# A three-pass float32 convolution network on one core: longer DRAM rows for three intermediate tensors, and the last pass's first layer in two halves instead of three thirds

## The chip, the cores and the metric

The kernel runs on one NeuronCore of a Trainium2 chip. The metric is the device time of one execution in microseconds. All data are float32. Engines are named as the profile names them: PE is TensorE's matmul, PEld its weight load, DVE VectorE, ACT ScalarE, POOL GpSimd, SP SyncE.

## What is computed

The input x is 8 x 96 x 96 x 192 (image, row, column, channel). Two residual layers follow, each on a group-normalised copy of its input (32 groups per image).

```
# layer 0
p     = gn(x) @ W_in + b_in                       # 192 -> 384
local = depthwise 3x3 conv(p)
mixed = local + 0.25 * (four running averages of local along rows and columns)
x1    = x + (layernorm(mixed) * g + b) @ W_out + b_out     # 384 -> 192
# layer 1
y     = depthwise 7x7 conv(gn(x1)) + bias
y     = gelu(layernorm(y) @ w0 + b0)              # 192 -> 768
x2    = x1 + gamma * (y @ w1 + b1)                # 768 -> 192
```

## The kernel before, in words

The program is one function, `conv_blocks_kernel`, with five stages one after the other; each writes an intermediate tensor to DRAM that the next one reads. The order of the instructions of each engine is the order of the program text (`tc.manual_schedule()`), and semaphores are put in where one engine's result is another's input or where a buffer is used again.

1. Projection (to about 750 us): group statistics of x, transposes, W_in, store to `P_d`.
2. The 3x3 convolution and the running averages (to about 1840 us): `P_d` to `M_d`.
3. LayerNorm and W_out (to about 2910 us): `M_d` to x1, which is stored twice. `finish_c` stores the sum in pixel order to `X2_d` (rows of 48 KB: one per image pair, column residue modulo 3 and image row), 3 KB of a row at a time from 96 partitions. `store_c` stores the channel-first copy `x1c` to `X1_d` (rows of 48 KB, every third one for one residue, so 144 KB from partition to partition), 3 KB of a row at a time. The last row of `X1_d` is a row of zeros, written in stage 1 from `pad`.
4. The 7x7 convolution (about 2910 to 3500 us): 16 rounds. `load_d` brings six channels of `X1_d` into `xin`, in runs of 1536 B: 64 rows, 48 KB apart, into partitions 0 to 63 by SyncE, and 64 more into partitions 64 to 127 by GpSimd; likewise the `band` of kernel weights. `scale_d` normalises on VectorE (L1009), `conv_d` runs the matmuls (L1024), ScalarE adds the bias into `yo` (L1035), and `store_d` writes `yo` to `Y_d` (L1064 from GpSimd; in the last round also L1063 from SyncE). A row of `Y_d` holds 4 image pairs x 2 column halves x 192 channels x 32 pixels, 192 KB, written in runs of 768 B.
5. The last pass (from about 3520 us): 24 loads of `y`, each 96 rows of 24 KB that lie 576 KB apart (L1116), and 96 units of 4 columns, four to a load. A unit u goes through these steps, which the loop at the end of the function interleaves over three neighbouring units:

   - `stats_e`, `norm_e`: LayerNorm of the unit on VectorE, with a power on GpSimd (L29)
   - `turn_in(u, k)`, k = 0, 1, 2: four transposes into one PSUM bank `pt` (L1169), which VectorE copies to `yT` (L1173)
   - `first_layer(u, mb)`, mb = 0, 1, 2: two of the six 128-column blocks of the hidden layer for both halves of the channels' pixels. The 192 channels are split as 128 + 64, so each of 4 sums, in a PSUM bank `hp` each, is a matmul over 128 rows (L1186) and one over 64 rows (L1196). The two 64-row matmuls of one block use different rows of the array. ScalarE then takes the GELU of each bank (L1205)
   - `second_layer(u, k)`, k = 0, 1, 2: 12 matmuls of 192 columns into one bank `po` (L1216), VectorE adds the residual `r` from `X2_d` (L1223), and GpSimd issues two stores of the output

   In the loop, thirds are interleaved: first_layer(u, k), turn_in(u + 1, k), statistics or norm of unit u + 2, second_layer(u - 1, k). [...] two for `pt`, four for `hp`, two for `po`.

A float32 matmul appears in the trace as two matmul records and two weight loads.

Of the kernel before, what the change touches and what calls it, by code (L numbers as in the profile page):

```python
# [8 lines left out]
F32 = mybir.dt.float32  # L9
# [3 lines left out]
PSUM = bass.MemoryType.PSUM  # L13
# [71 lines left out]
def conv_blocks_kernel(  # L85
# [31 lines left out]
    nc = tc.nc  # L117
    B, S, _, D = x.shape
# [4 lines left out]
    NE = EXP // 128  # L123
# [16 lines left out]
    PH = 3  # L140
    WV = S // PH

    X1_d = dram.tile([BP * S * PH + 1, D, WV, 2], F32, name="X1_d")
    X2_d = dram.tile([BP, PH, S, WV, 2, D], F32, name="X2_d")
    NV = 2
    WQ = WV // NV

    Y_d = dram.tile([S * PH, BP, NV, D, 2 * WQ], F32, name="Y_d")


    ZL = 2 * RB + 2
# [69 lines left out]
    with ExitStack() as ph:  # L221
# [68 lines left out]
        def store_kernels():  # L290
            nc.sync.dma_start(
                Z0_d.rearrange("(m p) t l -> p m (t l)", p=128),
                z0.rearrange("p m t l -> p m (t l)"),
            )

            nc.sync.dma_start(Z1_d.rearrange("(i c) p l -> c i p l", c=S), z1)
            nc.sync.dma_start(
                X1_d[BP * S * PH].rearrange("(i c) v b -> i (c v b)", i=S), pad
            )

        NK = RB // WA
# [435 lines left out]

    def load_d(m):
        c = m * HC
        row = D * WV * 2  # L740
        pool = d_pools[m % ND > 0]
        xin = pool.tile([128, NT, BP, HC, 2 * WV], F32, tag="xin", name="xin")

        for t in range(NT):
            for g, eng in enumerate((nc.sync, nc.gpsimd)):
                src = bass.AP(
                    tensor=X1_d.tensor,
                    offset=X1_d.offset + (2 * t + g) * HG * PH * row + c * WV * 2,
                    ap=[[row, 64], [S * PH * row, BP], [1, HC * WV * 2]],
                )  # L750
                eng.dma_start(
                    xin[g * 64 : (g + 1) * 64, t].rearrange("q a c n -> q a (c n)"), src
                )
        band = pool.tile([128, HC, ZW], F32, tag="band", name="band1")
        for g, eng in enumerate((nc.sync, nc.gpsimd)):
            eng.dma_start(
                band[g * 64 : (g + 1) * 64].rearrange("q c l -> q (c l)"),
                Z2_d[:, c : c + HC].rearrange("r c l -> r (c l)"),
            )
        return band, xin  # L760
# [4 lines left out]
    with ExitStack() as ph:  # L765
# [85 lines left out]
        def finish_c(x1c, part, w, pos, rs, xr):  # L851
            x1u = sp.tile([S, WB, 2, D], F32, tag="x1u", name="x1u", bufs=3)
            for j in range(WB):
                for b in range(2):
                    k = 2 * j + b
                    nc.vector.scalar_tensor_tensor(
                        x1u[:, j, b],
                        pos[j][:S, b, :D],
                        rs[:, k : k + 1],
                        xr[:, b, j],  # L860
                        ALU.mult,
                        ALU.add,
                    )

            nc.gpsimd.dma_start(
                X2_d[part // NH, part % NH, :, w : w + WB].rearrange("h v b c -> h (v b c)"),
                x1u.rearrange("h v b c -> h (v b c)"),
            )
            nc.vector.tensor_copy(
                x1c[:, :, w : w + WB].rearrange("h c v b -> h (v b) c"),  # L870
                x1u.rearrange("h v b c -> h (v b) c"),
            )
# [118 lines left out]
    with ExitStack() as ph:  # L991
# [51 lines left out]
        def store_d(yo, i):  # L1043
            for bl in range(NB):

                pieces = [(3, HB - 3)]
                if bl == 0:
                    pieces.append((HB - 3, HB))
                if bl == NB - 1:
                    pieces.append((0, 3))  # L1050
                for k in range(2):
                    c = i * CD + k * HC
                    for lo, hi in pieces:
                        r = (S - HB - bl * HG) * PH
                        src = yo[k * 64 + lo * PH : k * 64 + hi * PH, bl]
                        dst = Y_d[r + lo * PH : r + hi * PH, :, :, c : c + HC].rearrange(
                            "r b a c n -> r (b a) (c n)"
                        )
                        src = src.rearrange("r a c n -> r a (c n)")

                        n = NV if i == D // CD - 1 else 0
                        if n:
                            nc.sync.dma_start(dst[:, :n], src[:, :n])  # L1063
                        nc.gpsimd.dma_start(dst[:, n:], src[:, n:])  # L1064
# [25 lines left out]

    WH = 4
    WE = 2 * WH
    HE = 128 // WH
    with ExitStack() as ph:
        ip = ph.enter_context(tc.tile_pool(name="e_in", bufs=2))
        sp = ph.enter_context(tc.tile_pool(name="e_small", bufs=3))
        tp = ph.enter_context(tc.tile_pool(name="e_t", bufs=2))
        ps_t = ph.enter_context(tc.tile_pool(name="e_ps_t", bufs=2, space=PSUM))  # L1100
        ps_h = ph.enter_context(tc.tile_pool(name="e_ps_h", bufs=4, space=PSUM))
        ps_o = ph.enter_context(tc.tile_pool(name="e_ps_o", bufs=2, space=PSUM))

        def place(n):
            bp, n = divmod(n, PH * NV)
# [7 lines left out]
        def load_y(n):  # L1113
            bp, p, a = place(n)
            ys[n] = ip.tile([S, D, 2 * WQ], F32, tag="y", name=f"y_{n}")
            nc.sync.dma_start(ys[n], Y_d[PH - 1 - p :: PH, bp, a])  # L1116

        def load_r(u):
            n, t = divmod(u, per)
            bp, p, a = place(n)  # L1120
            v = a * WQ + t * WH
            rs_[u] = ip.tile([128, S // HE, 2 * D], F32, tag="r", name="r", bufs=4)
            for k in range(S // HE):
                nc.sync.dma_start(
                    rs_[u][:, k],
                    X2_d[bp, p, k * HE : (k + 1) * HE, v : v + WH].rearrange(
                        "h v b c -> h v (b c)"
                    ),
                )

        def bias_r(u):
            r = rs_[u].rearrange("p k (b c) -> p (k b) c", b=2)
            nc.gpsimd.tensor_tensor(
                r, r, b1g.unsqueeze(1).to_broadcast([128, 2 * S // HE, D]), ALU.add
            )
# [41 lines left out]
        def first_layer(u, mb):  # L1177
            if mb == 0:
                gs[u] = tp.tile([128, NE, 2, WH * S], F32, tag="g", name="g")
            yT, g = yTs[u].rearrange("p k h j -> p k (h j)"), gs[u]  # L1180
            ms = (2 * mb, 2 * mb + 1)
            hps = {}
            for m in ms:
                for q in range(2):
                    hps[m, q] = ps_h.tile([128, WH * S], F32, tag="hp", name="hp")
                    nc.tensor.matmul(  # L1186
                        hps[m, q],
                        w0w[:, 2 * q, m * 128 : (m + 1) * 128],
                        yT[:, 2 * q],
                        start=True,  # L1190
                        stop=False,
                    )
            for m in ms:
                for q in range(2):
                    p = slice(q * DH, (q + 1) * DH)
                    nc.tensor.matmul(  # L1196
                        hps[m, q],
                        w0w[p, 1, m * 128 : (m + 1) * 128],
                        yT[p, 1],
                        start=False,  # L1200
                        stop=True,
                    )
            for m in ms:
                for q in range(2):
                    nc.scalar.activation(  # L1205
                        g[:, m, q], hps[m, q], AF.Gelu, bias=b0g[:, m : m + 1], scale=1.0
                    )

        def second_layer(u, k):
            if k == 0:  # L1210
                xos[u] = tp.tile([128, S // HE, 2, D], F32, tag="xo", name="xo")
            g, xo = gs[u], xos[u]
            po = ps_o.tile([128, 2, D], F32, tag="po", name="po")
            for q in range(2):
                for m in range(NE):
                    nc.tensor.matmul(  # L1216
# [22 lines left out]
        with tc.manual_schedule():  # L1239
# [8 lines left out]
                    for k in range(3):  # L1248
                        turn_in(0, k)
            for u in range(n_u + 1):  # L1250
                for k in range(3):
                    if u < n_u:
                        first_layer(u, k)
                    if u + 1 < n_u:
                        turn_in(u + 1, k)
                    if k == 0:
                        if u + 1 < n_u:
                            load_r(u + 1)
                        if u < n_u:
                            bias_r(u)  # L1260
                    if u + 2 < n_u:
                        if k < 2:
                            for j in range(4 * k, 4 * k + 4):
                                stats_e(u + 2, j)
                        else:
                            for j in range(WE):
                                norm_e(u + 2, j)
                    if u >= 1:
                        second_layer(u - 1, k)


# [45 lines left out]
```

## Time and profile before

6009.42 us, the median of three runs (6007.35 to 6020.1). The profiled execution took 6009.9 us.

| engine | busy us | share of the span |
|---|---|---|
| PE | 5680.5 | 95% |
| PEld | 3943.4 | 66% |
| DVE | 3454.0 | 57% |
| POOL | 2634.7 | 44% |
| ACT | 2440.3 | 41% |

The costliest groups of the last pass on PE are L1216 (1178.3 us busy), L1186 (794.4 us) and L1196 (449.4 us). The page's slices show tenths of busy time per fortieth of the span (150 us each): PE is at 9 tenths or full everywhere but in the slices of the 7x7 convolution, where it is at 6 or 7, and the DMA engines are at 9 or full there. Matmul records overlap, since a matmul's end is modelled: what a matmul costs is read from the distance of the starts, and not from the durations. The table of windows gives busy time, granted clock and DMA traffic per stretch; its DMA share can go a little over 1.

### The profile page before, as it was taken

The page shows a single profiled execution, that of the slowest core. Times are in us where ns is not written, and L with a number is a line of the kernel's source. Part 1 is how long each engine was busy: PE and PEld are TensorE (multiplying, and loading weights), DVE is VectorE, ACT ScalarE, POOL GpSimd, SP SyncE. Part 2 cuts the span into 40 slices and gives each one's busy share as a digit, 9 for nine tenths or more (in the row PEclk, how much of TensorE's full clock was granted, in tenths as well). Part 3 has the DMA queues.
Part 4 walks back from the last instruction along what each step waited for, and adds up shares of the span by engine and source line. Part 5 has one row for each costly group of instructions (what it writes and reads, how often), then busy time and mean ns, then how long its engine had stood idle before and what let it go on. Part 6 is the DMA issues. An engine that isn't in the chain of part 4 may idle for free.

```text
span 6009.9 us, 122810 instructions
## 1 busy us (share of the span) xinstructions
PE 5680.5 (95%) x48550; PEld 3943.4 (66%) x48550; DVE 3454.0 (57%) x8023; ACT 2440.3 (41%) x6146; POOL 2634.7 (44%) x2835
## 2 busy tenths in 40 slices
PE   6999989999998999999677769999999999999999
PEld 3655633333336989898666657777777777777777
DVE  5555469999995667777532334444444444444442
ACT  2444457777774555555333322222222222222221
POOL 1111148888886666666444422322332233233222
PEclk9999989999999999999888889999999999999999
DMA  7999779999987888888899952222222222222221
GB/s 206 282 285 258 219 213 243 244 242 244 244 231 210 266 261 268 262 267 261 232 286 290 284 141 69 66 72 63 79 64 78 64 79 64 78 64 77 61 64 37
DMA packets 570206, 1054.36 MB, mean 175 GB/s; under 512 B 109575, under 2 KB 426260, under 8 KB 567328
## 3 DMA queue, kind: packets, MB, share of 16 engines
q1 hardware_dynamic: 439344, 593.23, 37.8%
q0 software_dynamic: 124160, 450.67, 24.1%
q8 instruction: 384, 6.29, 0.5%
q10 hardware_dynamic: 6128, 2.61, 0.2%
q14 instruction: 190, 1.56, 0.1%
HBM read 585.19 MB, written 476.57 MB: 177 GB/s over the span
## 4 chain that ended last, share of the span: by engine, by line
PE 77%; DMA 6%; DVE 1%; issue 1%; SPq 1%; POOL 1%; ACT 0%; DVEq 0%; POOLq 0%; ACTq 0%
PE po L1216 19%; PE po L833 13%; PE hp L1186 12%; PE pl L579 10%; PE hp L1196 7%; PE pa L600 5%; PE pt L831 4%; DMA xin<-X_d 4%; PE py L1024 2%; PE pt L1169 2%; PE pa L603 2%; DMA Y_d<-yo 1%; DVE xin L1009 1%; DMA band<-Z_d 0%; SPq L1063 0%
## 5 line engine op out<-in xcount | busy, mean ns | idle before, releaser
L1205 ACT ACTIVATE g<-hp,b0g 128x384 f32<-128x384 f32 x1152 | 573.9, 580 | 1856.4 <-PE hp L1196 1856.4
L1216 PE MATMUL po<-w1g,g 128*128 128x192 f32 x6912 | 1178.3, 327 | 0.0
L1216 PEld LDWEIGHTS po<-w1g,g 128*128 128x128 f32 x6912 | 1116.6, 190 | 1.6 <-issue 1.1
L833 PE MATMUL po<-wc,mt 128*96 128x193 f32 x4608 | 912.8, 333 | 0.0
L1173 DVE COPY yT<-pt 128x384 f32<-128x384 f32 x288 | 251.4, 873 | 1126.7 <-PE pt L1169 1126.4
L1234 POOL DMA_DIRECT2D out_dram<-xo x576 | 321.3, 560 | 1147.9 <-DVE xo L1223 1119.4
L1186 PE MATMUL hp<-yT,w0w 128*128 128x384 f32 x2304 | 794.4, 488 | 0.4 <-ACT g L1205 0.4
L833 PEld LDWEIGHTS po<-wc,mt 128*96 128x96 f32 x4608 | 701.8, 163 | 68.6 <-ACT mean L837 65.0
L579 PE MATMUL pl<-pin,band 34*32 34x380 f32 (+1 forms) x13824 | 629.9, 489 | 19.3 <-DMA pin<-P_d 18.5
L1186 PEld LDWEIGHTS hp<-yT,w0w 128*128 128x128 f32 x2304 | 431.4, 191 | 231.6 <-issue 2.6
L609 DVE TENSOR_TENSOR_SCAN z<-decay,loc 128x768 f32<-128x768 f32 x288 | 505.9, 1756 | 61.2 <-ACT loc L588 31.7
L1024 PE MATMUL py<-xin,band 63*64 63x248 f32 (+1 forms) x6912 | 405.5, 394 | 138.3 <-DVE xin L1009 136.2
L649 POOL TENSOR_TENSOR mo<-mo,z 128x768 f32<-128x768 f32 x288 | 529.6, 1839 | 3.3 <-ACT mo L604 0.4
L618 DVE TENSOR_TENSOR_SCAN z<-decay,z 128x768 f32<-128x768 f32 x288 | 498.2, 1730 | 0.0
L579 PEld LDWEIGHTS pl<-pin,band 34*32 34x32 f32 x13824 | 232.8, 107 | 398.7 <-issue 397.1
L1024 PEld LDWEIGHTS py<-xin,band 63*64 63x64 f32 x6912 | 345.0, 142 | 198.5 <-DVE xin L1009 123.5
L840 ACT ACTIVATE sq<-pt,mean 96x384 f32<-96x384 f32 x768 | 443.0, 577 | 25.7 <-ACT mean L837 0.8
L1196 PE MATMUL hp<-yT,w0w 64*128 64x384 f32 x2304 | 449.4, 508 | 0.0
L600 PE MATMUL pa<-loc,mix 128*32 128x384 f32 x3456 | 431.9, 493 | 0.0
L603 PE MATMUL pa<-last,down 96*32 96x384 f32 x1152 | 426.9, 493 | 0.9 <-ACT mo L604 0.9
L29 POOL TENSOR_TENSOR rs<-rs_ve,neg_half 96x8 f32<-96x8 f32 x96 | 158.6, 1652 | 606.3 <-DVE rs_ve L28 606.3
L362 PE MATMUL pm<-xT,win 128*128 128x384 f32 x1152 | 395.9, 494 | 3.3 <-DVE po L386 3.3
(116 smaller groups left out, 7707.4 us busy)
## 6 DMA issues: line engine op xcount, KB each, us to landing
P_d<-po POOLq DMA_DIRECT2D x96, 1152.0 KB, 9.9
pin<-P_d SPq DMA_DIRECT2D x192, 576.0 KB
mt<-M_d SPq DMA_DIRECT2D x576, 192.0 KB
xq<-in_x_dram SPq DMA_DIRECT2D x96, 576.0 KB
xr<-in_x_dram SPq DMA_DIRECT2D x384, 144.0 KB
X_d<-x1u POOLq DMA_DIRECT2D x192, 288.0 KB, 4.2
X_d<-x1c SPq DMA_DIRECT2D x192, 288.0 KB
y<-Y_d SPq DMA_DIRECT2D x24, 2304.0 KB
```

Of the source, the lines that this page charges most:

```text
L579: nc.tensor.matmul(pls[g][at * RB : (at + 1) * RB, :, lo:hi], band[rows, c, kh, :], pin[rows, c, :, NJ - 1 - j, lo + kh - 1 : hi + kh - 1] ...
L600: nc.tensor.matmul(pa[at], mix[:, i, at], loc[:, q], start=True, stop=True)
L603: nc.tensor.matmul(pa[at], down[:, to], last[:, q], start=True, stop=True)
L609: nc.vector.tensor_tensor_scan(zf, decay_f, loc.rearrange("p q n -> p (q n)"), 0.0, ALU.mult, ALU.add)
L618: nc.vector.tensor_tensor_scan(zr, decay_f, zr, 0.0, ALU.mult, ALU.add)
L649: nc.gpsimd.tensor_tensor(m, m, z, ALU.add)
L833: nc.tensor.matmul(po[:S, b], lhs[m], wc[:, m], start=(m == 0), stop=(m == NC - 1))
L1024: nc.tensor.matmul(pys[t // 2][g][k * 64 : (k + 1) * 64, t % 2, :, lo:hi], pair[k][0][rows, c, d * ZS : d * ZS + 64], pair[k][1][rows, t, ...
L1186: nc.tensor.matmul(hps[m, q], w0w[:, 2 * q, m * 128 : (m + 1) * 128], yT[:, 2 * q], start=True, stop=False,)
L1196: nc.tensor.matmul(hps[m, q], w0w[p, 1, m * 128 : (m + 1) * 128], yT[p, 1], start=False, stop=True,)
L1205: nc.scalar.activation(g[:, m, q], hps[m, q], AF.Gelu, bias=b0g[:, m : m + 1], scale=1.0)
L1216: nc.tensor.matmul(po[:, q], g[:, m, q, k * 128 : (k + 1) * 128], w1g[:, m], start=(m == 0), stop=(m == NE - 1),)
```

## The change

It has two parts.

The first makes each row of three DRAM tensors 4 KB (1024 float32 values) longer: `X1_d` rows go from 48 to 52 KB (as 16 unused channels), `X2_d` rows from 48 to 52 KB, `Y_d` rows from 192 to 196 KB. The added part is neither written nor read; only the distance between rows changes. It is meant to keep rows that are moved together from lying at distances with many factors of two.

The second part reorders the last pass. `first_layer` is called for two halves of the hidden layer, three blocks of 128 columns each, instead of three thirds; six PSUM banks are filled at a time. To have the banks, `pt` gets one buffer instead of two, and `po` shares a pool of seven with `hp`. The new loop body is written out: half a first layer, a transpose group, a third of a second layer, a transpose group, the other half of the first layer, a transpose group, and the other two thirds of the second layer. Its purpose is to change less often between matmuls over 128 rows and matmuls over 64 rows.

```diff
+    NP = 1024
+    DP = D + NP // (2 * WV)
+    X1_d = dram.tile([BP * S * PH + 1, DP, WV, 2], F32, name="X1_d")
+    X2_d = dram.tile([BP, PH, S, WV * 2 * D + NP], F32, name="X2_d")
...
+    Y_d = dram.tile([S * PH, BP * NV * D * 2 * WQ + NP], F32, name="Y_d")
+    Y_v = Y_d[:, : BP * NV * D * 2 * WQ].rearrange(
+        "r (b a c n) -> r b a c n", a=NV, c=D, n=2 * WQ
+    )
...
-        row = D * WV * 2
+        row = DP * WV * 2
...
-        ps_t = ph.enter_context(tc.tile_pool(name="e_ps_t", bufs=2, space=PSUM))
-        ps_h = ph.enter_context(tc.tile_pool(name="e_ps_h", bufs=4, space=PSUM))
-        ps_o = ph.enter_context(tc.tile_pool(name="e_ps_o", bufs=2, space=PSUM))
+        ps_t = ph.enter_context(tc.tile_pool(name="e_ps_t", bufs=1, space=PSUM))
+        ps_h = ph.enter_context(tc.tile_pool(name="e_ps_h", bufs=7, space=PSUM))
...
-            ms = (2 * mb, 2 * mb + 1)
+            ms = range(mb * NE // 2, (mb + 1) * NE // 2)
...
-            po = ps_o.tile([128, 2, D], F32, tag="po", name="po")
+            po = ps_h.tile([128, 2, D], F32, tag="hp", name="po")
...
-                for k in range(3):
-                    if u < n_u:
-                        first_layer(u, k)
-                    if u + 1 < n_u:
-                        turn_in(u + 1, k)
...
-                    if u >= 1:
-                        second_layer(u - 1, k)
+                if u < n_u:
+                    first_layer(u, 0)
+                if u + 1 < n_u:
+                    turn_in(u + 1, 0)
+                    load_r(u + 1)
+                if u < n_u:
+                    bias_r(u)
+                if u + 2 < n_u:
+                    for j in range(4):
+                        stats_e(u + 2, j)
+                if u >= 1:
+                    second_layer(u - 1, 0)
+                if u + 1 < n_u:
+                    turn_in(u + 1, 1)
+                if u < n_u:
+                    first_layer(u, 1)
+                if u + 1 < n_u:
+                    turn_in(u + 1, 2)
+                if u + 2 < n_u:
+                    for j in range(4, WE):
+                        stats_e(u + 2, j)
+                if u >= 1:
+                    second_layer(u - 1, 1)
+                if u + 2 < n_u:
+                    for j in range(WE):
+                        norm_e(u + 2, j)
+                if u >= 1:
+                    second_layer(u - 1, 2)
```

The stores and loads of the three tensors are rewritten to the new row lengths and otherwise move the same bytes in the same order.

More of the change, by code (lines that the diff above doesn't have):

```diff
@@ L141, in conv_blocks_kernel @@
     WV = S // PH
-    X1_d = dram.tile([BP * S * PH + 1, D, WV, 2], F32, name="X1_d")
-    X2_d = dram.tile([BP, PH, S, WV, 2, D], F32, name="X2_d")
+    NP = 1024
+    DP = D + NP // (2 * WV)
+    X1_d = dram.tile([BP * S * PH + 1, DP, WV, 2], F32, name="X1_d")
+    X2_d = dram.tile([BP, PH, S, WV * 2 * D + NP], F32, name="X2_d")
     NV = 2
     WQ = WV // NV
-    Y_d = dram.tile([S * PH, BP, NV, D, 2 * WQ], F32, name="Y_d")
+    Y_d = dram.tile([S * PH, BP * NV * D * 2 * WQ + NP], F32, name="Y_d")
+    Y_v = Y_d[:, : BP * NV * D * 2 * WQ].rearrange(
+        "r (b a c n) -> r b a c n", a=NV, c=D, n=2 * WQ
+    )
     ZL = 2 * RB + 2
@@ L297, in store_kernels @@
             nc.sync.dma_start(
-                X1_d[BP * S * PH].rearrange("(i c) v b -> i (c v b)", i=S), pad
+                X1_d[BP * S * PH, :D].rearrange("(i c) v b -> i (c v b)", i=S), pad
             )
@@ L865, in finish_c @@
             nc.gpsimd.dma_start(
-                X2_d[part // NH, part % NH, :, w : w + WB].rearrange("h v b c -> h (v b c)"),
+                X2_d[part // NH, part % NH, :, w * 2 * D : (w + WB) * 2 * D],
                 x1u.rearrange("h v b c -> h (v b c)"),
@@ L1055, in store_d @@
                         src = yo[k * 64 + lo * PH : k * 64 + hi * PH, bl]
-                        dst = Y_d[r + lo * PH : r + hi * PH, :, :, c : c + HC].rearrange(
+                        dst = Y_v[r + lo * PH : r + hi * PH, :, :, c : c + HC].rearrange(
                             "r b a c n -> r (b a) (c n)"
@@ L1115, in load_y @@
             ys[n] = ip.tile([S, D, 2 * WQ], F32, tag="y", name=f"y_{n}")
-            nc.sync.dma_start(ys[n], Y_d[PH - 1 - p :: PH, bp, a])
+            nc.sync.dma_start(ys[n], Y_v[PH - 1 - p :: PH, bp, a])
         def load_r(u):
@@ L1125, in load_r @@
                     rs_[u][:, k],
-                    X2_d[bp, p, k * HE : (k + 1) * HE, v : v + WH].rearrange(
-                        "h v b c -> h v (b c)"
-                    ),
+                    X2_d[
+                        bp, p, k * HE : (k + 1) * HE, v * 2 * D : (v + WH) * 2 * D
+                    ].rearrange("h (v n) -> h v n", n=2 * D),
                 )
@@ L1250, in conv_blocks_kernel @@
             for u in range(n_u + 1):
-                for k in range(3):
-                    if u < n_u:
-                        first_layer(u, k)
-                    if u + 1 < n_u:
-                        turn_in(u + 1, k)
[L1256 to L1267, printed above, removed]
-                    if u >= 1:
-                        second_layer(u - 1, k)
+                if u < n_u:
[26 more added lines that the diff above has]
+                    second_layer(u - 1, 2)
 _INS = [
```

## The prediction

> **What bounds the kernel now.** I read the page's 40 slices first, then a table of windows over the last two passes, then the instruction groups of the last pass, its timeline, and the waits of the convolution pass. The windows (end columns: granted clock, DMA share, GB/s):
>
> ```profile
> core 0: us, PE busy (x) PEld busy (x) DVE busy (x) ACT busy (x) POOL busy (x), PEclk, DMA share, GB/s
> 2905.00:3500.00 595.00, 433.04 (x7066) 370.09 (x7068) 190.35 (x403) 212.15 (x427) 251.22 (x383) 0.84 0.98 267
> 3500.00:3575.00 75.00, 27.61 (x108) 14.16 (x100) 31.73 (x81) 10.63 (x21) 20.04 (x21) 0.66 0.58 142
> 3575.00:5999.00 2424.00, 2423.15 (x12581) 1814.38 (x12580) 1092.70 (x2896) 566.27 (x1137) 718.07 (x761) 1.00 0.24 68
> ```
>
> The last pass (third row, 2424 us) is TensorE from end to end: 2423 us busy, clock 1.00, DMA share 0.24. The convolution pass (first row) has TensorE idle for 27% while the DMA engines are full. A faster transfer can thus shorten the convolution pass and the hand-over after it, but not the last pass; a shorter PE sequence can shorten the last pass almost one for one. The first 2900 us touch the padded tensors only through the stores of x1 in the LayerNorm pass (PE share 9 tenths and more), where a store hides.
>
> Inside the last pass a third of a unit looks like this (timeline, PE alone; start, duration):
>
> ```profile
> 4058.33 4.09 PE L1216 MATMUL po<-w1g,g 128*128 128x192 f32 x24
> 4062.26 2.74 PE L1186 MATMUL hp<-yT,w0w 128*128 128x384 f32 x8
> 4064.93 1.56 PE L1196 MATMUL hp<-yT,w0w 64*128 64x384 f32 x8
> 4066.43 0.55 PE L1169 MATMUL pt<-ident,yn 96*128 96x96 f32 x4
> 4066.81 4.09 PE L1216 MATMUL po<-w1g,g 128*128 128x192 f32 x24
> ```
>
> From start to start it takes 8.48 us: 3.93 + 2.67 + 1.50 + 0.38. (A float32 matmul is two records.) 96 units of three thirds are 2442 us, the length of the pass. The starts of the single records in this stretch give the undisturbed spacing: 162.5 ns for a record of the second layer, 322.5 ns for a 128-row record of the first, 322.5 ns for a pair of 64-row records (the two halves run side by side, 7 ns apart), 82.5 ns for a transpose. What exceeds it lies around the 64-row block: the step into it takes 416 ns instead of 322.5 (+93), its four pairs hold one of 427 ns instead of 322.5 (+104), the step out takes 413 instead of 315.5 (+98), the first transpose's step 138 instead of 82.5 (+56), and the second record after the transposes 192 instead of 162.5 (+30). Together 381 ns a third, 96 x 3 x 0.381 = 110 us of the pass. Check: 2424 us less the undisturbed spacings of the records in it (6912 x 0.1625 + 2272 x 0.3225 + 1136 x 0.3225 + 1125 x 0.0825 = 2315) leaves 109.
>
> [...] the 381 ns sit where rows go from 128 to 64 and back. [...] Our pitches are 48, 144, 192 and 576 KB[...]; the trace has y (576 KB pitch) at 1677 ns for 24 KB, 70 ns per KB, beside 66 for x at 72 KB pitch in the first 45 us. [...] no PE wait on a bank shows in the last pass (idle 0.5 us in all).
>
> **The padding.** It adds no instruction and no byte moved. Does the pitch cost anything now? In the convolution pass each round takes 33.4 us for 192 x 384 KB of xin, 64 x 312 KB of band and 56.6 MB of Y over 16 rounds, 9.5 MB, or 286 GB/s. The waits there say that data come late:
>
> ```profile
> engine line waited for: us in total, times, longest us
> DVE xin L1009 <- DMA xin<-X_d: 349.0, 30, 23.4
> PE py L1024 <- DVE xin L1009: 129.7, 16, 20.2
> ```
>
> The rate alternates within a round (table of windows again):
>
> ```profile
> 3186.00:3199.00 13.00, 13.00 (x252) 11.27 (x248) 3.98 (x7) 7.26 (x14) 7.71 (x12) 1.00 1.03 347
> 3201.00:3209.00 8.00, 5.91 (x112) 4.74 (x104) 0.00 (x0) 4.21 (x8) 3.45 (x6) 1.00 1.05 207
> ```
>
> 347 GB/s while Y stores and SyncE's loads overlap, 207 while GpSimd's loads run alone. In the slow stretches only that queue moves, into partitions 64 to 127: packets of 4608 B take 368 ns (80 ns per KB). [...] The band packets of the same queue, from rows 156 KB apart, are as slow (382 ns for 4992 B). And the loads of pin in the 3x3 pass, rows 4.5 KB apart into 32 partitions[...], have a median of 341 ns for 4608 B, 76 per KB. Reads of the pixel-ordered x1 with its 48 KB pitch, spread over 128 partitions, have a median of 65 ns for 1536 B, 43 per KB. So the slow stretch follows the destination's partitions, which the padding leaves alone. Y's stores, pitch 192 KB, run at 188 ns for 4608 B in the fast stretch, which is fast already. What may be the pitch is the tail of Y's last stores (a sixth of their packets over 420 ns) and the 4 ns per KB of y. On the path these matter once, between the last convolution and the first transpose (40.6 us: Y stores 18, first y 13, statistics 7). I take 2 us there and 2 us over the 16 rounds: -4. Bounds: 0, and if all loads ran at 347 GB/s, 9.5 MB in 27.4 us, 6 us x 15 rounds = -90. Side effect: rows of Y no longer touch, so a store of 360 runs of 768 B becomes 45 rows of 8; the bytes and the run length stay.
>
> **The halves.** Per unit the first layer goes from three blocks of 4 groups to two of 6; its 24 + 24 records, 72 of the second layer and 12 transposes stay. One block of 64-row matmuls less saves 381 ns. Two joints are new: second layer to transposes, and transposes to a 128-row block; [...] the trace does not show them. Bounds: 0, or the 56 and 30 ns that such joints cost elsewhere; I take 30. So 0.35 us x 96 = -34 us (range -28 to -37). The start of the pass gains too: PE waits 3.5 us for yn before the second unit's transposes, and with six groups before them instead of four part of that is filled: -2.
>
> **New waits.** One transpose bank instead of two: the next turn_in waits for the copy of the last. In the new order a unit runs (us) first half to 6.0, turn 6.5, second layer 10.4, turn 10.75, first half to 16.75, turn 17.2, second layer twice to 25.1. The turns are at least 4 us apart and a copy takes 0.87: no wait. Queued behind a waiting transpose would be all of PE, so this counts. Seven banks shared by 12 hp and 3 po per unit: each tile comes back seven allocations later. The second half's hp tiles (from 10.75) need the first half's GELUs, six at 0.5 us from about 4.7, done by 8. The second po needs the first one's sum, done at 11. The tightest are the two late sums: the last waits in VectorE's queue behind eight norm_e (8 x 0.464) that wait for the 1.65 us power on GpSimd, so it ends about 27, 2 us into the next unit; its bank is wanted by the next unit's first po at 31.5. VectorE has 13.3 us of work in a unit of 25, so nothing piles up. norm_e ends at about 26.4, and its transposes come at 31.5. Cost: 0.
>
> **Sum.** 6009.4 - 34 - 2 - 4 = 5969.
>
> **Rivals.** (a) The pitch does bind in part, loads or Y stores gaining 1 to 5 us a round: 15 to 75 us more, 5890 to 5954. For it: data come late in every round. [...] Fully, 5969 + 4 - 90 = 5883. (b) A wait takes the place of the switch: if the shared banks or the late sum hold PE for 1 us a unit, +96 on top of -40, 6065; if a copy's 0.87 us shows once a unit, 6053. For it: one copy, then all of PE behind it. Against: the 2 us and more of slack in each step above. (c) [...] the halves save nothing and the joints cost up to 0.09 x 96 = 8, 6003 to 6014. Against: within the block the later pairs stand at 322.5 ns.
>
> **Chances.** Main case 0.72 (5955 to 5985), (a) 0.16, (b) 0.07, (c) 0.05. The range runs from 5915, which takes in most of (a), to 5986; it leaves out (b), (c) and the far end of (a), about 0.17. Faster by over 12 us: main and (a), 0.88; the same 0.05; slower 0.07.
>
> **What would show it.** Units of 25.1 us instead of 25.44 in the timeline; one 64-row block less per unit, each still with its 0.38 us; no PE idle time before L1169's and L1186's successors named DVE or ACT; GpSimd's loads still near 207 GB/s and rounds still near 33 us. Rounds near 28 us would prove the pitch argument wrong, and PE gaps in the last pass the one on waits.

## The result, and the profile after

The changed kernel takes 5984.55 us (median of four runs, 5982.8 to 5990.22) beside 6012.9 us for the kernel before: ratio 0.9954, 95% interval 0.9937 to 0.9971, about 28 us less. The profiled executions took 6009.9 and 5981.3 us, 28.6 us apart. By the starts of the PE records this splits as follows.

| stretch | before us | after us | difference |
|---|---|---|---|
| start to the first 7x7 matmul | 2963.6 | 2963.8 | +0.2 |
| 7x7 convolution, first to last matmul | 537.0 | 533.6 | -3.4 |
| last of these to the first transpose | 41.0 | 42.2 | +1.2 |
| last pass, first transpose to last matmul | 2456.3 | 2429.6 | -26.7 |
| to the end | 12.1 | 12.1 | 0.0 |

The gain is in the last pass. The table of windows of the changed kernel, same stretches as before, shows no other picture than before: the last pass is full of PE work at full clock, the convolution pass is full of DMA work.

```profile
2905.00:3500.00 595.00, 433.19 (x7076) 366.97 (x7074) 190.96 (x404) 214.23 (x431) 258.58 (x388) 0.84 0.97 267
3500.00:3575.00 75.00, 27.35 (x90) 14.76 (x92) 27.15 (x74) 7.20 (x14) 15.24 (x17) 0.64 0.55 137
3575.00:5970.00 2395.00, 2391.94 (x12584) 1834.72 (x12580) 1098.38 (x2903) 558.43 (x1140) 743.17 (x762) 1.00 0.24 69
```

One unit of the last pass in the timeline of the changed kernel, PE alone (start, duration):

```profile
4509.74 4.09 PE L1222 MATMUL po<-w1g,g 128*128 128x192 f32 x24
4513.67 0.49 PE L1175 MATMUL pt<-ident,yn 96*128 96x96 f32 x4
4514.00 4.06 PE L1192 MATMUL hp<-yT,w0w 128*128 128x384 f32 x12
4517.99 2.21 PE L1202 MATMUL hp<-yT,w0w 64*128 64x384 f32 x12
4520.13 0.55 PE L1175 MATMUL pt<-ident,yn 96*128 96x96 f32 x4
4520.52 7.99 PE L1222 MATMUL po<-w1g,g 128*128 128x192 f32 x48
4528.35 4.03 PE L1192 MATMUL hp<-yT,w0w 128*128 128x384 f32 x12
4532.31 2.21 PE L1202 MATMUL hp<-yT,w0w 64*128 64x384 f32 x12
4534.45 0.55 PE L1175 MATMUL pt<-ident,yn 96*128 96x96 f32 x4
4534.84 0.35 PE L1222 MATMUL po<-w1g,g 128*128 128x192 f32 x1
```

From L1222 at 4509.74 to the same place at 4534.84 are 25.10 us; over the pass the median is 25.09, against 25.44 before. There are two 64-row blocks (L1202) per unit instead of three. Each holds six pairs instead of four, and still pays its steps: by the starts of the single records 416 ns into it, 427 ns for one of its pairs, 413 ns out of it. The waits of the last pass in the changed kernel have no PE row at all (the three longest, the rest cut):

```profile
engine line waited for: us in total, times, longest us
ACT g L1211 <- PE hp L1202: 1805.5, 188, 11.4
DVE yT L1179 <- PE pt L1175: 1029.4, 186, 5.6
POOL out_dram L1240 <- DVE xo L1229: 819.4, 186, 9.7
...
```

ScalarE and VectorE wait for PE, GpSimd for VectorE, and PE for none of them: seven shared banks and one transpose bank are enough once the pass runs. In the convolution pass the same two waits as before are long, and within a round the rate still falls to about 210 GB/s (waits, then windows):

```profile
DVE xin L1015 <- DMA xin<-X_d: 342.4, 30, 21.8
...
PE py L1030 <- DVE xin L1015: 126.6, 16, 21.0
```

```profile
3200.00:3208.00 8.00, 4.69 (x91) 3.66 (x82) 0.00 (x0) 3.80 (x8) 1.33 (x2) 0.95 1.02 210
3212.00:3228.00 16.00, 14.82 (x240) 12.45 (x244) 6.00 (x10) 6.27 (x12) 9.04 (x14) 0.83 1.05 337
```

### The profile page after: what moved, and what is told of

It is laid out like the page before. It is cut to its first block, busy times and chain, and to the rows that moved or that the text cites. A ratio compares the mean times of both kernels' runs of the same rounds, so it can differ in the third digit from the quotient of the medians.

```text
span 5981.3 us, 122717 instructions
## 1 busy us (share of the span) xinstructions
PE 5648.4 (94%) x48550; PEld 3960.0 (66%) x48550; DVE 3455.5 (58%) x8023; ACT 2431.9 (41%) x6146; POOL 2662.8 (45%) x2835
## 4 chain that ended last, share of the span: by engine, by line
PE 77%; DMA 7%; DVE 1%; issue 1%; SPq 1%; POOL 1%; ACT 0%; POOLq 0%; DVEq 0%; ACTq 0%
PE po L1222 19%; PE po L839 13%; PE hp L1192 12%; PE pl L585 10%; PE hp L1202 7%; PE pa L606 5%; PE pt L837 4%; DMA xin<-X_d 4%; PE pa L609 2%; PE py L1030 2%; PE pt L1175 2%; DMA band<-Z_d 1%; DMA Y_d<-yo 1%; DVE xin L1015 0%; SPq L1069 0%
## 5 line engine op out<-in xcount | busy, mean ns | idle before, releaser
L1222 PE MATMUL po<-w1g,g 128*128 128x192 f32 x6912 | 1161.3, 327 | 0.0
L1222 PEld LDWEIGHTS po<-w1g,g 128*128 128x128 f32 x6912 | 1120.3, 190 | 1.1 <-issue 1.1
L1192 PE MATMUL hp<-yT,w0w 128*128 128x384 f32 x2304 | 781.6, 489 | 0.4 <-DVE yT L1179 0.4
L1240 POOL DMA_DIRECT2D out_dram<-xo x576 | 344.8, 601 | 875.8 <-DVE xo L1229 848.6
L1202 PE MATMUL hp<-yT,w0w 64*128 64x384 f32 x2304 | 423.5, 500 | 0.0
```

The costliest lines, as they stand in the source:

```text
L1192: nc.tensor.matmul(hps[m, q], w0w[:, 2 * q, m * 128 : (m + 1) * 128], yT[:, 2 * q], start=True, stop=False,)
L1202: nc.tensor.matmul(hps[m, q], w0w[p, 1, m * 128 : (m + 1) * 128], yT[p, 1], start=False, stop=True,)
L1222: nc.tensor.matmul(po[:, q], g[:, m, q, k * 128 : (k + 1) * 128], w1g[:, m], start=(m == 0), stop=(m == NE - 1),)
```

## The experiments

The theory after the result: the whole gain comes from one 64-row block less per unit, at a fixed cost per block; the longer rows do nothing, because the loads of the convolution pass are held back by the partitions they write and not by the distance of the rows they read; and the start of the last pass gave some of the gain back. The rival on the first part is a cost per pair of 64-row matmuls; on the second, a share of the longer rows in the gain.

### One part alone

`pad_only` is the kernel before with the longer rows (NP = 1024), and its last pass in thirds. `halves_only` is the changed kernel with rows as short as before:

```diff
-    NP = 1024
+    NP = 0
```

> The kernel before with the 4 KB longer rows alone; the last pass keeps its thirds. Theory (the pitch costs nothing, the slow stretches of the convolution pass are set by the partitions that a load writes): within 4 us of before, about 6009, rounds of the convolution still 33 us, GpSimd's loads still about 205 GB/s. Rival (the pitch binds in part): 10 us or more faster than before, and the halves alone are that much slower than the whole change.

Measured: 6014.69 us beside 6014.76 for the kernel before, ratio 0.9999, interval 0.999 to 1.0007. The longer rows bring no gain that can be seen. The interval reaches from 6 us less to 4 us more, so the rival's 10 us are ruled out, and a few microseconds are not.

> The reordered last pass alone, rows as long as before. Theory: the whole gain, 28 us faster than before (about 5984), with 25.09 us a unit. Rival (the pitch binds in part): less than 20 us faster.

Measured: 5983.66 us, ratio 0.9948, interval 0.9936 to 0.9961; units of 25.09 us. The halves alone bring all of the gain that these runs can resolve. The 3.4 us of the convolution pass in the table above are within the scatter: with the short rows that pass was 537.0, 539.6 and 540.4 us long in three profiles, with the long rows 533.6 to 546.6 in five.

### More blocks instead of fewer

`sixths` is the kernel before with the first layer in six blocks. Work and data stay; each unit has six 64-row blocks instead of three.

```diff
-            ms = (2 * mb, 2 * mb + 1)
+            ms = (mb,)
...
-                        first_layer(u, k)
+                        first_layer(u, 2 * k)
+                        first_layer(u, 2 * k + 1)
```

> The kernel before with the first layer in six blocks instead of three: the same matmuls, three more 64-row blocks per unit. Theory (a fixed cost per 64-row block): each more block costs the step in, the long pair and the step out, 0.093 + 0.104 + 0.098 = 0.295 us, or up to 0.38: 3 x 96 x 0.295 to 0.38 = 85 to 110 us slower, about 6095 to 6120. Rival (the cost goes with the pairs of 64-row matmuls, whose number stays): within 10 us of before.

Measured: 6124.63 us, ratio 1.0182, interval 1.0168 to 1.0196, 110 us more than before. The timeline of one third:

```profile
4502.19 1.45 PE L1186 MATMUL hp<-yT,w0w 128*128 128x384 f32 x4
4503.58 0.92 PE L1196 MATMUL hp<-yT,w0w 64*128 64x384 f32 x4
4504.42 1.56 PE L1186 MATMUL hp<-yT,w0w 128*128 128x384 f32 x4
4505.91 0.92 PE L1196 MATMUL hp<-yT,w0w 64*128 64x384 f32 x4
4506.76 0.55 PE L1169 MATMUL pt<-ident,yn 96*128 96x96 f32 x4
```

The number of pairs is as before, and the time went with the number of blocks: the rival on pairs falls. A unit takes 26.63 us, 1.19 more than 25.44 for three more blocks, 0.397 us each. That is a little more than the 0.295 to 0.38 expected. The blocks show why: the four 128-row records that follow a 64-row block take 1.49 us to the next start, those that follow the second layer 1.38 (4502.19 to 4503.58). So the way back costs 0.10 us more, one long step after the switch, when a 128-row matmul and not a transpose comes next. With 6, 3 and 2 blocks the units are 26.63, 25.44 and 25.09 us: 0.40 and 0.35 per block. What these runs show is the price of a block; what the engine does in that time, they do not show.

### What the distance of rows and the choice of partitions do to a load

`rows` leaves out the computation and only loads, always in runs of 1536 B from the same tensor; then 24 KB rows into 96 partitions.

```diff
+    def phase(name, n_dma, parts, pitch, engs=(nc.sync,)):
+        ...
+                for eng, (lo, hi) in zip(engs * len(parts), parts):
+                    src = rows(384 * (i % 8), pitch, hi - lo, 240 * pitch, 4, 384)
+                    eng.dma_start(t[lo:hi], src)
...
+    phase("l48", 16, low, 48 * KB)
+    phase("h48", 16, high, 48 * KB)
...
```

> Leaves out the whole computation and writes one small tile of output: only loads, in runs of 1536 B out of x as it lies in DRAM, 16 loads of four runs per row in each stretch, with the distance of the rows and the partitions as the only differences. Stretches: 64 partitions 0-63 with rows 48 KB apart, 64-127 with 48, 0-63 with 52, all 128 with 48, with 52, the two halves at once from SyncE and GpSimd with 48 and with 52, 0-63 with 64 KB; then 24 KB rows into 96 partitions, 576 and 580 KB apart. Theory (the partitions set the rate): about 210 to 225 GB/s for every 64-partition stretch whatever the distance, over 300 for 128 partitions, 280 or more for the two halves at once, 52 and 48 within 3% of each other, 576 and 580 within 5%. Rival (the distance of the rows sets it): 52 KB clearly faster than 48 and 64 the slowest, 128 partitions no faster than 64, 580 clearly faster than 576.

Its table of windows, one row per stretch in the order of the expectation (columns: stretch, length, DVE and POOL busy, granted clock, DMA share, GB/s):

```profile
4.00:28.00 24.00, 0.00 (x0) 0.00 (x0) 1.00 1.10 213
36.00:64.00 28.00, 0.00 (x0) 0.00 (x0) 1.00 1.10 204
70.00:96.00 26.00, 0.00 (x0) 0.00 (x0) 1.00 1.10 214
104.00:132.00 28.00, 0.00 (x0) 0.00 (x0) 1.00 1.06 373
140.00:168.00 28.00, 0.00 (x0) 0.00 (x0) 1.00 1.06 374
178.00:220.00 42.00, 0.00 (x0) 7.43 (x12) 1.00 1.06 260
230.00:272.00 42.00, 0.00 (x0) 7.43 (x12) 1.00 1.07 259
280.00:308.00 28.00, 0.00 (x0) 0.00 (x0) 1.00 1.10 205
314.00:370.00 56.00, 0.00 (x0) 0.00 (x0) 1.00 1.01 223
378.00:438.00 60.00, 0.00 (x0) 0.00 (x0) 1.00 1.00 220
```

Rows 48 or 52 KB apart give 213 and 214 GB/s into partitions 0 to 63, 373 and 374 into all 128, and 260 and 259 into both halves at once from two queues. Rows 64 KB apart give 205, and 576 against 580 KB 223 against 220. Going from 64 to 128 partitions gave 1.75 times the rate here (213 and 373 GB/s). For these loads the distance of the rows is out as the cause of the low rate, and the partitions that one transfer writes decide it. (The transfers over 128 partitions are also twice as large, 768 KB. Size alone does not bring the rate: the loads of the last two stretches have 2304 KB each, at 223 and 220 GB/s.) The number of partitions alone does not explain all of it: two queues writing one half each reach 260 GB/s, not the 280 expected, and are far from the 373 of one transfer over 128 partitions, and 96 partitions get hardly more (223 and 220) than 64 (204 to 214). The cause of both stays open, and so does why 64 partitions get less than 128. Each stretch was measured once.

### Where the convolution pass could gain

If the loads of one half, alone, are the slow part of a round, then their order should matter. All four kernels below start from the change with two transpose banks (`two_banks`, below). In `act_loads` and `sync_loads` another engine issues the loads for partitions 64 to 127:

```diff
-        for g, eng in enumerate((nc.sync, nc.gpsimd)):
+        for g, eng in enumerate((nc.sync, nc.scalar)):   # act_loads; sync_loads: (nc.sync, nc.sync)
```

> The change with two transpose banks, and the loads of the convolution pass for partitions 64-127 issued by ScalarE instead of GpSimd, which keeps only the stores of Y. Theory (the slow stretches are one half's loads alone, held back behind the stores in GpSimd's queue): the two halves now arrive together at 280 GB/s or more, rounds of 28 to 31 us instead of 33, 30 to 75 us faster than the change, 5910 to 5955. Rival (the round is bound by the bytes, at about 286 GB/s in any order, or by ScalarE waiting to issue): rounds of 33 us or more, 5980 or above.

Measured: 6117.0 us, ratio 1.017 (1.0155 to 1.0186), rounds of 43.1 us (the mean of the rounds after the first, here and below; in the changed kernel it is 32.5). The rate did come, and was lost again by waiting (windows, then timeline):

```profile
3200.00:3224.00 24.00, 10.10 (x160) 9.20 (x156) 4.74 (x8) 5.99 (x12) 6.56 (x11) 0.72 1.04 370
3224.00:3236.00 12.00, 12.00 (x233) 12.00 (x229) 4.75 (x8) 6.32 (x12) 1.94 (x4) 1.00 0.11 28
```

```profile
3203.46 0.59 ACTq L757 DMA_DIRECT2D xin<-X_d  x1
...
3213.04 0.58 ACTq L757 DMA_DIRECT2D xin<-X_d  x1
...
3216.26 1.63 ACT L1041 ACTIVATE yo<-py,dwb 128x512 f32<-128x512 f32 x3 [19.86 <-DMA Y_d<-yo]
...
3217.00 1.11 PE L1030 MATMUL py<-xin,band 63*64 63x256 f32 x2 [13.90 <-ACT yo L1041]
```

For 24 us the DMA engines move 370 GB/s, with both halves and the stores in flight, and then nearly nothing for 12. ScalarE's queue needs 10.16 us for three loads, the first and the last of which are shown. To issue one takes it only 0.6 us; in the trace's semaphore records the second and the third each start 0.02 us after an earlier load of the same queue has landed, so it is this wait that holds the queue. Meanwhile ScalarE takes no result out of PSUM, and PE waits 13.90 us for it. The theory on the rate holds, its round time is wrong: it left out what its rival named, ScalarE waiting to issue. ScalarE did no other work in that time; its activation at 3216.26 comes after 19.86 us of idle time.

> As the last, but SyncE issues the loads of both halves, one after the other. Theory: within the one queue only one half is written at a time, so loads alone stay at 205 to 225 GB/s, but the stores of Y can run beside them all the time; 6 MB of loads a round at 205 to 225 GB/s are 27 to 29 us, rounds of 29 to 32 us, 15 to 60 us faster than the change. Rival (the round is bound by the bytes): 33 us, no gain.

Measured: 5992.92 us, ratio 0.9972 (0.9961 to 0.9982), rounds of 33.7 us: no gain, and the theory's figure missed. The stores of a round come in one go, once ScalarE is through, and are issued within half a round; after that the loads run alone again, at 215 to 238 GB/s in three such stretches. `interleaved` spreads the stores instead: each load on GpSimd's queue is preceded by one or two stores of the round before.

```diff
+                if g:
+                    between()          # one or two steps of the last round's store_d
                 eng.dma_start(
...
-                store_d(yo, i)
+                todo = store_d(yo, i)  # now a list of steps
```

> The change with two transpose banks, and in GpSimd's queue of the convolution pass each load is preceded by one or two stores of Y of the round before, instead of all stores first and then all loads. Theory (what slows a round is that one half's loads run alone[...] at 205 GB/s): the stores now run beside the loads, 9.5 MB at 300 to 330 GB/s, rounds of 29 to 32 us, 15 to 60 us faster than the change. Rival (the round is bound by bytes in any order): 33 us, no gain.

Measured: 5919.44 us, ratio 0.9838 (0.9825 to 0.9851), rounds of 28.8 us. The same 430 us of the convolution pass, first in the changed kernel and then interleaved:

```profile
3000.00:3430.00 430.00, 332.91 (x5696) 279.90 (x5691) 128.29 (x214) 165.96 (x316) 200.47 (x308) 0.87 1.05 292
```

```profile
3000.00:3430.00 430.00, 380.52 (x6526) 335.88 (x6522) 141.65 (x236) 186.68 (x363) 232.80 (x348) 0.92 1.04 320
```

PE is busy for 381 instead of 333 us of them, and the DMA engines move 320 instead of 292 GB/s at almost the same share (1.05 and 1.04). Among GpSimd's packets of 4608 B the slow ones, over 330 ns, go from 30% to 7%. This kernel beats both: 68 us less than the changed kernel beside it (5987.29), and so more than the 15 to 60 us expected. How much comes from stores that run beside the loads, and how much from loads that no longer stand behind all the stores, this run does not separate.

`interleaved_short` asks whether the longer rows matter at this higher rate (NP = 0):

> The interleaved kernel with rows as short as before the change (NP = 0). Theory (the distance of the rows never sets the rate, not even where the DMA engines move 320 GB/s and more): within 5 us of the interleaved kernel, ratio to before about 0.984. Rival[...]: 10 us or more slower than with the longer rows, 0.986 or above.

Measured: 5919.46 us, ratio 0.9843 (0.9827 to 0.986), rounds of 28.9 us. No difference shows.

### The start of the last pass

Twelve transposes open the pass, and unit 0 and unit 1 have little to overlap with. From the first transpose to the start of the third unit it is 60.28 us, against 54.33 before. The table of windows for this stretch, before and after, and for a part of it after:

```profile
3541.00:3596.00 55.00, 47.73 (x205) 30.43 (x206) 38.29 (x94) 13.24 (x25) 12.39 (x9) 0.88 0.19 54
3539.00:3600.00 61.00, 49.74 (x205) 32.91 (x206) 38.09 (x93) 13.04 (x25) 12.67 (x9) 0.84 0.17 49
3560.00:3565.60 5.60, 5.60 (x12) 3.17 (x11) 2.36 (x7) 0.00 (x0) 0.00 (x0) 0.50 0.00 0
```

With the same number of records PE is idle for 11.3 us instead of 7.3 and busy for 49.7 instead of 47.7: two thirds of the loss are waiting, one third is slower work. The timeline of the changed kernel there:

```profile
3543.09 0.90 PE L1175 MATMUL pt<-ident,yn 96*128 96x96 f32 x4 [0.92 <-DVE yT L1179]
3544.91 0.90 PE L1175 MATMUL pt<-ident,yn 96*128 96x96 f32 x4 [0.92 <-DVE yT L1179]
...
3559.52 0.90 PE L1175 MATMUL pt<-ident,yn 96*128 96x96 f32 x4 [0.92 <-DVE yT L1179]
3560.21 6.75 PE L1192 MATMUL hp<-yT,w0w 128*128 128x384 f32 x12
...
3577.57 0.27 PE L1175 MATMUL pt<-ident,yn 96*128 96x96 f32 x1 [1.36 <-DVE yn L1160]
...
3579.92 5.47 PE L1222 MATMUL po<-w1g,g 128*128 128x192 f32 x24
```

Three times PE waits 0.92 us for the copy out of the one transpose bank. Transposes of unit 2 wait for yn, whose statistics now stand behind a copy that VectorE awaits for 7.16 us. The first half at 3560.21 takes 6.75 us where the steady pass has 4.06 (granted clock 0.50 over most of it, third row of the table), and the second layer at 3579.92 takes 5.47 instead of 4.09. These records follow idle times; that the idle times bring the lower clock is not shown, since no run varies them alone. `two_banks` gives the transposes their second bank back:

```diff
-        ps_t = ... name="e_ps_t", bufs=1 ...
-        ps_h = ... name="e_ps_h", bufs=7 ...
+        ps_t = ... name="e_ps_t", bufs=2 ...
+        ps_h = ... name="e_ps_h", bufs=6 ...
```

> The change with two transpose banks again and six banks shared by hp and po instead of seven. Theory: the 6 us by which the start of the last pass missed its forecast come from the single transpose bank (three waits of 0.92 us for a copy before and in the first unit)[...]; with two banks 2 to 6 us faster than the change, 5979 to 5982, units still 25.09 us, since a bank then comes back six allocations later and each is free by then. Rival (the seventh shared bank is needed): units longer than 25.09 us, slower than the change.

Measured: 5989.85 us, ratio 0.9953 (0.994 to 0.9965), units of 25.09 us. Six shared banks are enough, but the total did not fall. The next two ran beside each other to tell why.

> The changed kernel once more, beside the next one on the same chip: about 0.995 of before.

> The change with two transpose banks, beside the changed kernel. Theory (its last pass was 6 us shorter from the first transpose on, and what hid it in the total is the scatter of the convolution pass): 2 to 8 us faster than the change. Rival (the convolution pass ends later because of the two banks): the same time as the change.

Measured: 5987.29 us for the change (0.9948, 0.9935 to 0.996) and 5988.22 for two banks (0.9953, 0.9939 to 0.9966). The expected 2 to 8 us are not there. In the traces the last pass from first transpose to last matmul is 2429.6, 2429.8 and 2426.9 us long with one bank (the changed kernel, `halves_only`, `change_again`) and 2423.9 and 2426.6 with two, so the second bank is worth some 3 us there. All of this lies at the start: from the third unit to the last matmul it is 2369.3 us in each of the five, and 2402.0 in the kernel before. Counted from the first transpose, PE is idle at the start for 9.7 to 10.5 us with one bank and 6.8 to 8.0 with two, against 6.6 before. The rest of the difference goes with the time at the lower clock, which is not the same from one profile of a kernel to the next: in two profiles of the changed kernel the clock was at 0.50 for 19.2 and 16.7 us of the start, which took 60.28 and 57.61 us. In the total 3 us would hardly be seen: the convolution pass ahead varied from 533.6 to 546.6 us over the same profiles, and was longest in one with two banks; whether that is scatter alone stays open.

## Why the prediction was right, and where it was off

It forecast 5969 us and 40 us gained; 5984.55 came out, 28 us gained, inside its range of 5915 to 5986, but by only 1.5 us. That is luck in part: the same kernel measured again took 5987.29 (`change_again`), which lies outside. The gain, 28 us there and 31 in the repeat, is 0.7 to 0.8 of the forecast. Point by point:

**One 64-row block less, 0.35 us a unit.** Right to the digit: 25.44 to 25.09. From the third unit on, 94 units, it is 32.7 us (2402.0 to 2369.3). The joints cost what was taken for them: the steps from the second layer to the transposes and from those to the 128-row block are undisturbed (162.5 and 82 ns), and the 128-row block after transposes is 0.03 us longer (3.99 against 3.96 us).

**The cost is fixed per block.** Right, by `sixths` and `halves_only`: 0.40 and 0.35 us per block. Rival (c), a cost per pair of matmuls, is out.

**New waits cost 0.** Right for the steady pass, where PE waits for nothing, even with six shared banks. Rival (b) did not come in the 94 steady units.

**The start of the pass, -2 us.** This is the step that failed. It counted only the wait for yn that more matmuls would fill, and that wait did become shorter (3.50 to 2.76 us). But measured the start is +6 us in the profile, 4 of them more waiting and 2 slower records: three waits for the single transpose bank, which the step on new waits had ruled out for the spacing of the steady pass only; a later yn for unit 2; and the lower clock. Of these only the bank was tested, and it accounts for about 3 us. 32.7 less 6.0 is the 26.7 us that the last pass gained.

**The padding, -4 us.** No gain shows (0.9999, interval 0.999 to 1.0007), which was the near bound; 4 us lie inside that interval, so this small size is neither confirmed nor refuted. Rival (a), 15 us and more, is out by `pad_only`. The argument behind it, that the partitions decide and not the distance of the rows, is borne out by `rows`: 213, 214 and 205 GB/s into 64 partitions with rows 48, 52 and 64 KB apart, 373 and 374 into 128 with 48 and 52. But the number of partitions does not explain every rate there, and no run shows why fewer partitions are slower. The slow entry of the y loads, 70 ns per KB, was the one sign that pointed to pitch; 576 and 580 KB gave 223 and 220 GB/s, so no cost of the pitch shows there either; larger pitches were not run.

The start alone is 8 of the 12 us between the forecast gain of 40 and the 28 measured. The steady units brought 1 us less than the 34 taken for all 96. The rest is the size of the padding's term, but the scatter of the convolution pass is larger than that. (The rest of the distance from 5969 to 5984.55 is the kernel before, at 6012.9 us in this comparison and 6009.4 in the forecast.) Two sums of the forecast are slightly off, without weight for the outcome: 5969 less 75 is 5894, not 5890, and 368 ns for 4608 B are 82 ns per KB, not 80, if a KB is 1024 B as in its other figures.

## What to carry to other kernels

Look in the PE timeline for steps that are longer than the steady spacing and come with each change of the kind of matmul, multiply by their number, and group the matmuls so that there are fewer. Here the gain of the steady part was foretold to within a few per cent that way (34 us, measured 32.7); the start of the pass was not. Before padding rows, see whether a slow transfer follows the rows it reads or the partitions it writes; here the remedy lay in the order of loads and stores, worth more than twice the change itself (68 us beside 28). Check a buffer that is taken away also at the start of a pass, where the distances of the steady state do not hold.

## What was not expected of the hardware

- Two queues that load one half of the partitions each moved 260 GB/s together, far below the 373 of one transfer over 128 partitions.
- When a 128-row matmul and not a transpose follows a 64-row block, the second record after the switch is 0.10 us late as well, so that each of the three further blocks of `sixths` costs 0.397 us.
- Loads in ScalarE's queue held ScalarE: it took 0.6 us to issue a load of 384 KB, but 10.16 us for three, of which the second and the third each started 0.02 us after an earlier load had landed.
- Where GpSimd issued no loads (`act_loads`, `sync_loads`), the program ended 5 us after the start of its last matmul instead of 12. The time lies in the last long DRAIN of GpSimd's queue, 2.50 us there and 9.65 in the changed kernel; why it takes longer stays open.
